# Layer 3 of a four-layer graph network: the neighbour sums as seven products of halves, with the combinations of adj made by accumulating DMAs

## The chip, the cores and the metric

The kernel runs on one core of one Trainium2 chip. A core has a matrix engine (PE, fed by weight loads PEld), three engines for elementwise work (DVE, ACT and POOL, which is GpSimd) and a queue engine SP that issues transfers. All transfers, whichever engine issues them, run on the core's 16 DMA engines. The metric is the device time of one execution in microseconds, as a median over runs.

## The reference

The input is x (16 graphs of 1024 nodes with 256 features) and adj (16 dense matrices of 1024 by 1024). Four layers follow one another; each takes h = relu(layernorm(x)), computes a graph function of h and adj, and adds it to x. The change is in the last one, layer 3:

```
h = relu(layernorm(x))
agg = epsilon * h + adj @ h                     # the sums over neighbours
g = silu(rmsnorm(agg @ W1 + b1))                # inner product, 256 -> 1024
x = x + g @ W2 + b2                             # outer product, 1024 -> 256
```

Everything is float32. epsilon * h is had by adding epsilon to adj's diagonal.

## The kernel before, in words

Layer 3 is written out for 16 batches (graphs) in `layer_3`, one after the other, with the stages of two neighbouring batches interleaved by hand. A scheduler orders each engine's instructions from that program text; every engine then works through its own queue in order, and waits where an operand or a buffer is not ready.

For one batch:

- `load(b)` (L1130) queues the loads on SP: x, h's earlier part hn, and adj transposed in two halves of 1024 rows by 512 columns, `at[b][0]` (left) and `at[b][1]` (right). A half is 2 MB, loaded by four DMAs of 512 KB (L1146). Only three buffers exist for such halves (two named bxt, one named at), so a half of batch b+2 is loaded into a buffer that batch b or b+1 has given back.
- `prepare(b)` (L1149) adds epsilon to the diagonal blocks on POOL (L1154, four small adds for each half), adds the layer's input on DVE (L1163), takes the statistics (L1166, L1167), 1/sqrt on POOL (L83, tile rs), and normalises on ACT into h (L1173, eight instructions). POOL adds b2 to x (L1177).
- `sums(b)` (L1182) makes agg transposed, tile ag, in four parts: for each half of adj's columns and each half of the 256 features, eight matmuls of 128x512 (L1189) into one PSUM tile named ph. ACT copies each to ag (L1191). Four DVE subtractions (L1195 to L1199) make the combinations tt that the next stage needs.
- `inner(ag, tt)` (L1203) is the product with W1. It is already done as seven products of halves in place of eight (Winograd's form of Strassen's scheme): 28 matmuls of 128x512 (L1210), with DVE to combine (L1229, L1231, L1214), ACT to square (L1216) and POOL to sum the squares (L1218, tiles ss, from two buffers named sq).
- `norm` turns the sums of squares with PE (`mean`, L1250), makes 1/rms on POOL (L83, tile rms), spreads it with PE (`spread`, L1258), and multiplies and applies silu on DVE and ACT (L1261, L1262).
- `outer` (L1265) is the product with W2, also as seven products: 112 matmuls of 128x128 (L1279), with the combinations made on DVE (L1273). It uses a buffer s1 of 1 MB. `prepare(b + 2)` is put in the middle of it.
- The result is stored by one DMA issued on POOL (L1337).

In iteration b the order of work is: inner of b, then the four parts of sums of b+1 with mean and spread of b between them (parts 0, mean, 1, spread, 2, 3), then outer of b with prepare of b+2. So the sums of a batch stand in one stretch of the matrix engine's queue, between inner and outer of the batch before it. The first batch has no such cover: its sums stand alone, at the end of layer 2.

Of the kernel before, what the change touches and what calls it, by code (L numbers as in the profile page):

```python
# [9 lines left out]
F32 = mybir.dt.float32  # L10
AF = mybir.ActivationFunctionType
ALU = mybir.AluOpType
# [4 lines left out]
P = 128  # L17
B, N, D, H = 16, 1024, 256, 1024
NT = N // P
DC = D // P  # L20
# [20 lines left out]
def gnn_stack(ctx: ExitStack, tc: tile.TileContext, a: dict, out: bass.AP):  # L41
    nc = tc.nc
# [29 lines left out]
    def rows(ap):  # L72
        return ap.rearrange("(t p) d -> p t d", p=P)
# [1019 lines left out]
    def layer_3(shared, x, hn, at, h, eye):  # L1093
        with ExitStack() as st:
            wp = st.enter_context(tc.tile_pool(name="w3", bufs=1))
            big = st.enter_context(tc.tile_pool(name="big3", bufs=2))
# [16 lines left out]
            NH = 512  # L1113
# [3 lines left out]
            a11, a12, a21, a22 = (w1[:, c, p * HH * P : (p + 1) * HH * P] for p in range(2) for c in range(2))  # L1117
            nc.gpsimd.tensor_tensor(ws[:, 0], a21, a22, ALU.add)
            nc.gpsimd.tensor_tensor(ws[:, 1], ws[:, 0], a11, ALU.subtract)
            nc.gpsimd.tensor_tensor(a21, a11, a21, ALU.subtract)  # L1120
            nc.gpsimd.tensor_tensor(ws[:, 2], a12, ws[:, 1], ALU.subtract)

            wt = wp.tile([P, 3, HH, P], F32, name="wt")
# [6 lines left out]
            def load(b):  # L1130
# [7 lines left out]
                while len(at[b]) < N // NH:  # L1138
# [7 lines left out]
                        nc.sync.dma_start(half[:, t : t + 2], rows(a["adjT"][b])[:, t : t + 2, n0 : n0 + NH])  # L1146
                    at[b].append(half)

            def prepare(b):  # L1149

                def diagonal(half):
                    for t in range(half * NT // 2, (half + 1) * NT // 2):
                        own = at[b][half][:, t, t * P % NH : t * P % NH + P]
                        nc.gpsimd.tensor_tensor(own, own, eye, ALU.add)  # L1154
                part = slice(0 if b else NT - 1, NT)
                if b:
                    diagonal(0)
                    h[b] = hn[b]
                tiles = range(NT)[part]
                mv = small.tile([P, NT, 2], F32, name="mv")  # L1160
                for t in tiles[::2]:
                    two = slice(t, min(t + 2, NT))
                    nc.vector.tensor_add(x[b][:, two], x[b][:, two], hn[b][:, two])  # L1163
                    for t in range(NT)[two]:
                        st = small.tile([P, 6], F32, name="st", bufs=4)
                        nc.vector.bn_stats(st, x[b][:, t])  # L1166
                        nc.vector.bn_aggr(mv[:, t], st)  # L1167
                n = len(tiles)
                rs = inv_sqrt(small, mv[:, part, 1], LN_EPS, [P, n], "rs")
                shift = small.tile([P, n], F32, name="shift")  # L1170
                nc.vector.scalar_tensor_tensor(shift, mv[:, part, 0], -1.0, rs, op0=ALU.mult, op1=ALU.mult)
                for k, t in enumerate(tiles):
                    nc.scalar.activation(h[b][:, t], x[b][:, t], AF.Relu, bias=shift[:, k : k + 1], scale=rs[:, k : k + 1])  # L1173
                diagonal(1)
                to = x[b] if b else big.tile([P, NT, D], F32, name="x", bufs=3)
                for t in range(0, NT, 2):
                    nc.gpsimd.tensor_tensor(to[:, t : t + 2], x[b][:, t : t + 2], b2[:, None].to_broadcast([P, 2, D]), ALU.add)  # L1177
                x[b] = to

            def sums(b):  # L1180

                ag = big.tile([P, DC, N], F32, name="ag", bufs=1)  # L1182
                tt = big.tile([P, 4, NH], F32, name="tt", bufs=1)
                b21 = []

                def part(n0, c):
                    pa = psum.tile([P, NH], F32, name="ph", bufs=5)
                    for mt in range(NT):
                        nc.tensor.matmul(pa, h[b][:, mt, c * P : (c + 1) * P], at[b][n0 // NH][:, mt],  # L1189
                                         start=mt == 0, stop=mt == NT - 1)  # L1190
                    nc.scalar.copy(ag[:, c, n0 : n0 + NH], pa)  # L1191
                    if (n0, c) == (0, 1):
                        b21.append(pa)
                    if (n0, c) == (NH, 0):
                        nc.vector.tensor_sub(tt[:, 0], pa, ag[:, 0, :NH])  # L1195
                    if (n0, c) == (NH, 1):
                        nc.vector.tensor_sub(tt[:, 1], pa, tt[:, 0])
                        nc.vector.tensor_sub(tt[:, 2], pa, ag[:, 0, NH:])
                        nc.vector.tensor_sub(tt[:, 3], b21[0], tt[:, 1])  # L1199
                return (ag, tt), [lambda n0=n0, c=c: part(n0, c) for n0 in range(0, N, NH) for c in range(DC)]  # L1200

            def inner(ag, tt):

                hh = [big.tile([P, HC, NH], F32, name=f"hh{q}", bufs=1) for q in range(2)]
                ss = [small.tile([P, NH], F32, name=f"ss{q}", bufs=1) for q in range(2)]
# [2 lines left out]
                def product(lhsT, rhs, onto=None):  # L1208
                    ph = onto if onto is not None else psum.tile([P, NH], F32, name="ph", bufs=5)
                    nc.tensor.matmul(ph, lhsT, rhs, start=onto is None, stop=True, skip_group_check=onto is not None)  # L1210
                    return ph
# [9 lines left out]
                left = lambda: None  # L1221
                for k in range(HH):
                    mine = slice(k * P, (k + 1) * P)
                    p1, u2, u3 = (small.tile([P, NH], F32, name=name) for name in ("p1", "u2", "u3"))
                    ph = product(a11[:, mine], ag[:, 0, :NH])
                    nc.scalar.copy(p1, ph)
                    left()
                    ph = product(ws[:, 1, mine], tt[:, 1])
                    nc.vector.tensor_add(u2, ph, p1)  # L1229
                    ph = product(a21[:, mine], tt[:, 2])  # L1230
                    nc.vector.tensor_add(u3, ph, u2)  # L1231
                    p5 = product(ws[:, 0, mine], tt[:, 0])
                    result(HH + k, 1, p5, u3)
                    result(HH + k, 0, product(a22[:, mine], tt[:, 3]), u3)
                    result(k, 0, product(a12[:, mine], ag[:, 1, :NH]), p1)
                    left = lambda k=k, mine=mine, p5=p5, u2=u2: result(
                        k, 1, product(ws[:, 2, mine], ag[:, 1, NH:], p5), u2)
                left()
                return hh, ss

# [72 lines left out]

            load(0)
            prepare(0)
            load(1)
            ags, parts = sums(0)
            for part in parts:
                part()
            prepare(1)  # L1320
            for b in range(B):
                if b + 2 < B:
                    load(b + 2)
                hh, ss = inner(*ags)
                mean, spread = norm(hh, ss)
                parts = [lambda: None] * 4
                if b + 1 < B:
                    ags, parts = sums(b + 1)
                parts[0]()
                mean()  # L1330
                parts[1]()
                spread()
                parts[2]()
                parts[3]()

                outer(b, hh, (lambda: prepare(b + 2)) if b + 2 < B else (lambda: None))
                nc.gpsimd.dma_start(rows(out[b]), x[b])  # L1337

    layers_0_1()
    with tc.tile_pool(name="shared", bufs=2) as shared:  # L1340
# [50 lines left out]
```

## Time and profile before

| | |
|---|---|
| time, median of 3 runs | 4616.06 us (4612.09 to 4619.73) |
| profiled execution, span | 4622.5 us |
| PE, busy share of the span | 94% |
| DVE, ACT, POOL, busy share | 55%, 28%, 35% |
| layer 3, from its first matmul to the last instruction | 3334.9 to 4616.8 us of the span |
| one batch of layer 3, steady | 78.3 us |
| DMA engines, mean busy share in slices 30 to 39 of the span | 0 to 3 tenths |

The span runs from the first to the last instruction's record in the profiled execution, and the profile gives no other time of it; it is 6.4 us above the median of the runs. The profile has these parts: busy time by engine; the span in 40 slices; the DMA queues; the chain of work that ended last, which is followed back from the last instruction to whatever released it; groups of like instructions with their mean time and what ended the idle time before them; and DMA issues with the time from issue to landing. The chain can also be listed in order of time, and each engine's instructions as a timeline. In such a line the first number is the start in us from the beginning of the span, the second how long it took, then the engine (SPq and POOLq are the queues that issue transfers), the tile and the line, and xN for N instructions merged. PE records a float32 matmul as two instructions.

### The profile page before, as it was taken

How to read it: one execution, taken by the hardware profiler on the slowest of the kernel's cores; microseconds unless marked ns; L12 is line 12 of the kernel's file. 1: busy time of each engine (PE TensorE's matmuls, PEld its weight loads, DVE VectorE, ACT ScalarE, POOL GpSimd, SP SyncE). 2: the span in 40 equal slices, each digit the busy share in tenths (PEclk: the TensorE clock that was granted, in tenths of full speed). 3: DMA queues.
4: the chain of work that ended last, by engine and by line, in shares of the span. 5: the costliest groups of instructions: out<-in, count | busy, mean ns of one | idle time of the engine just before them, and what ended most of it. 6: DMA issues, size and time to landing. Idle time of an engine off the chain costs nothing. (4 is left out here: it accounts for less than half of the span.)

```text
span 4622.5 us, 54868 instructions
## 1 busy us (share of the span) xinstructions
PE 4336.9 (94%) x19223; PEld 2956.2 (64%) x19223; DVE 2535.5 (55%) x6436; ACT 1279.5 (28%) x2741; POOL 1623.5 (35%) x1914
## 2 busy tenths in 40 slices
PE   8999799999997899999999999999799999999998
PEld 4444345555554687778787878787655656565656
DVE  6667944555554344444444444445356666676765
ACT  1111111221121232323232323233234333333333
POOL 3222333433333333332332323234244444445352
PEclk9999899999998999999999999999899999999999
DMA  4333244455544644454444454542142222232310
GB/s 150 112 116 100 73 112 146 164 194 188 156 145 154 196 138 154 131 166 141 154 121 151 131 159 135 167 144 73 55 142 89 100 92 92 88 104 82 110 46 19
DMA packets 530989, 576.78 MB, mean 125 GB/s; under 512 B 42544, under 2 KB 439472, under 8 KB 528304
## 3 DMA queue, kind: packets, MB, share of 16 engines
q1 hardware_dynamic: 499536, 460.27, 32.0%
q0 software_dynamic: 31040, 111.44, 6.9%
q8 instruction: 206, 3.38, 0.3%
q14 instruction: 207, 1.70, 0.1%
HBM read 469.65 MB, written 116.65 MB: 127 GB/s over the span
## 5 line engine op out<-in xcount | busy, mean ns | idle before, releaser
L295 PE MATMUL pa<-at,h 128*128 128x512 f32 x1088 | 495.3, 608 | 33.0 <-DVE ag L300 33.0
L295 PE MATMUL pa<-at,q 128*128 128x512 f32 x960 | 423.6, 594 | 0.0
L623 PE MATMUL pf<-hb,ab 128*128 128x256 f32 x1568 | 407.9, 383 | 14.5 <-DMA hb<-hs_d 5.7
L295 PEld LDWEIGHTS pa<-at,h 128*128 128x128 f32 x1088 | 209.7, 196 | 277.6 <-issue 231.5
L735 PE MATMUL pf<-hs,wx 128*128 128x256 f32 x1536 | 348.9, 381 | 19.2 <-POOL hs L726 17.6
L735 PEld LDWEIGHTS pf<-hs,wx 128*128 128x128 f32 x1536 | 290.6, 191 | 62.5 <-POOL hs L726 19.4
L623 PEld LDWEIGHTS pf<-hb,ab 128*128 128x128 f32 x1568 | 280.3, 191 | 67.2 <-issue 14.2
L295 PEld LDWEIGHTS pa<-at,q 128*128 128x128 f32 x960 | 178.2, 190 | 215.9 <-issue 212.8
L1189 PE MATMUL ph<-bxt,hb 128*128 128x512 f32 x704 | 310.8, 597 | 3.8 <-ACT hb L1173 3.0
L1218 POOL TENSOR_TENSOR ss<-ss,sq 128x512 f32<-128x512 f32 x224 | 280.7, 1271 | 87.1 <-ACT sq L1216 83.4
L1023 POOL DMA_INDIRECT hs_d<-h,table x128 | 129.6, 1013 | 330.0 <-ACTq L1009 150.8
L1279 PEld LDWEIGHTS po<-w,hh 128*128 128x128 f32 x2048 | 235.9, 193 | 9.5 <-issue 7.2
L1279 PE MATMUL po<-w,hh 128*128 128x128 f32 x2048 | 240.1, 277 | 1.4 <-ACT hh L1262 0.7
L1189 PEld LDWEIGHTS ph<-bxt,hb 128*128 128x128 f32 x704 | 133.2, 192 | 164.7 <-issue 159.8
L740 DVE TENSOR_TENSOR gates<-pf,bias 128x512 f32<-128x512 f32 x128 | 88.3, 691 | 238.6 <-PE pf L735 238.6
L1261 DVE TENSOR_TENSOR hh<-hh,po 128x512 f32<-128x512 f32 x256 | 154.5, 681 | 96.7 <-PE po L1258 96.7
L83 POOL TENSOR_TENSOR rs<-rs_v,mhalf 128x8 f32<-128x8 f32 (+1 forms) x65 | 106.9, 1645 | 255.0 <-DVE rs_v L79 241.5
L771 PE MATMUL pf<-bd,h 128*128 128x384 f32 (+4 forms) x512 | 185.6, 454 | 5.3 <-ACT bs L610 2.8
L1216 ACT ACTIVATE sq<-hh 128x512 f32<-128x512 f32 x224 | 141.1, 630 | 164.3 <-DVE hh L1214 125.6
L830 ACT ACTIVATE r<-pr 128x256 f32<-128x256 f32 (+3 forms) x230 | 68.1, 348 | 403.5 <-PE pr L789 389.5
L1214 DVE SCALAR_TENSOR_TENSOR hh<-ph,b,u 128x512 f32<-128x512 f32 x192 | 144.0, 751 | 64.9 <-PE ph L1210 54.8
L774 DVE TENSOR_TENSOR bxt<-bxt,pf 128x384 f32<-128x384 f32 (+4 forms) x256 | 125.0, 501 | 97.0 <-PE pf L771 95.5
(296 smaller groups left out, 8473.1 us busy)
## 6 DMA issues: line engine op xcount, KB each, us to landing
at<-in_adjT SPq DMA_DIRECT2D x64, 1024.0 KB, 7.1
ab<-in_adj SPq DMA_DIRECT2D x128, 512.0 KB, 4.3
bxt<-in_adjT SPq DMA_DIRECT2D x88, 512.0 KB, 6.7
at<-in_adjT SPq DMA_DIRECT2D x40, 512.0 KB, 6.8
ad<-in_adj SPq DMA_DIRECT2D x128, 128.0 KB, 6.2
x_d<-x POOLq DMA_DIRECT2D x16, 1024.0 KB, 5.1
he_d<-h POOLq DMA_DIRECT2D x16, 1024.0 KB, 8.9
heT_d<-hT POOLq DMA_DIRECT2D x16, 1024.0 KB, 4.2
```

Of the source, the lines that this page charges most:

```text
L295: nc.tensor.matmul(pa, h[:, mt, c * P : (c + 1) * P], at[n0 // 512][:, mt], start=mt == 0, stop=mt == NT - 1)
L623: nc.tensor.matmul(pb, ab[:, jts[k]], hb[:, jts[k]], start=k == 0, stop=k == len(jts) - 1)
L735: nc.tensor.matmul(pg[:, e], wx[:, c, q * D + e * P : q * D + (e + 1) * P], self.hs[:, c], start=c == 0, stop=c == DC - 1)
L771: nc.tensor.matmul(pf, h[:, g, c * P : (c + 1) * P], bd[:, g, b0 : b0 + n, S : S + far], start=True, stop=True)
L774: return lambda: nc.vector.tensor_add(to, to, pf)
L1023: nc.gpsimd.indirect_dma_start(out=hs_d[t][g][:, :], out_offset=row(1, g, t, s), in_=h[:, g], in_offset=None)
L1189: nc.tensor.matmul(pa, h[b][:, mt, c * P : (c + 1) * P], at[b][n0 // NH][:, mt], start=mt == 0, stop=mt == NT - 1)
L1214: nc.vector.scalar_tensor_tensor(hh[q][:, k], ph, b1[:, k : k + 1], u, op0=ALU.add, op1=ALU.add)
L1216: nc.scalar.activation(sq, hh[q][:, k], AF.Square)
L1218: nc.gpsimd.tensor_tensor(ss[q], ss[q], sq, ALU.add)
L1261: nc.vector.tensor_mul(hh[q][:, k], hh[q][:, k], pr)
L1279: nc.tensor.matmul(po[:, n], left[:, c, n * P : (n + 1) * P], right[:, c], start=onto is None and n == 0 and c == 0, stop=c == HH - 1, ski ...
```

## The change

Part one: the eight products of the sums become seven. With adj transposed cut in quarters b11 (left, first 512 rows), b12 (right, first 512 rows), b21 (left, last 512 rows) and b22 (right, last 512 rows), and h cut likewise, the kernel now makes p1 = m0 b11 and adds m1 b21 onto it, then p5, p7, p6, one product with b21's combination, and one with b22 onto p7: seven groups of four matmuls of 128x512, where there were four groups of eight.

Part two: this needs three combinations of quarters of adj, each of 128 partitions by 2048 elements (1 MB): t1 = b12 + b11, t3 = b12 + b22, b11 + t3, and b21 plus that; four adds in all. They are made by DMAs from SBUF to SBUF that add onto their destination, issued on GpSimd (`add_to`). b12 is overwritten by t1, so t3 starts from a second load of b12 (two DMAs of 512 KB on SP, new L1197) into the buffer s1 that outer uses.

Part three: the combinations of h (S1, S2, S4 and a21 in place) are four new DVE instructions of 128x512 elements for each batch. Behind the products, DVE does seven combinations where it did four, and ACT three copies where it did four.

Part four: the order. The diagonal of the right half, and the DMA for t1, move from `prepare(b + 2)` to the end of iteration b, behind the store of the output on POOL's queue (`first_sum`, under `issue_after`). The DMA for t3 belongs to `inner`; those onto b11 and b21 to the first and second part of the sums. In the built program each engine has this order between inner of b and outer of b: PE: four matmuls of p1, mean, four onto p1, four of p5, spread, four of p7, four of p6, four with b21, eleven of outer, four with b22, the rest of outer. POOL: store, four diagonal adds, the DMA for t1, the first add of squares of the next inner, the DMA for t3, the other thirteen adds of squares, the DMA onto b11, rms, the DMA onto b21, four diagonal adds of a left half, rs. DVE: the four combinations of h stand at the end of outer, before its last add to x. SP: the left half of b+3 (once the buffer of b+1's right half is free), then b12 again, then x, and the right half (once the left half of the batch before it is free).

For the first batch POOL's order is: the DMA for t1 (still in layer 2), layer 2's last scatters, the combinations of the weights, the copy of x, four diagonal adds, rs of batch 1, the DMA for t3, four adds of b2 to x of batch 1, the DMA onto b11, the DMA onto b21, then the DMA for t1 of batch 1, its diagonal, the DMA for t3, two adds of squares, four diagonal adds of batch 2's left half, and the other adds of squares.

The diff:

```diff
--- before.py
+++ after.py
@@ -1117,7 +1117,7 @@
             a11, a12, a21, a22 = (w1[:, c, p * HH * P : (p + 1) * HH * P] for p in range(2) for c in range(2))
             nc.gpsimd.tensor_tensor(ws[:, 0], a21, a22, ALU.add)
             nc.gpsimd.tensor_tensor(ws[:, 1], ws[:, 0], a11, ALU.subtract)
-            nc.gpsimd.tensor_tensor(a21, a11, a21, ALU.subtract)
+            nc.gpsimd.tensor_tensor(a21, a21, a11, ALU.subtract)
             nc.gpsimd.tensor_tensor(ws[:, 2], a12, ws[:, 1], ALU.subtract)
 
             wt = wp.tile([P, 3, HH, P], F32, name="wt")
@@ -1146,15 +1146,16 @@
                         nc.sync.dma_start(half[:, t : t + 2], rows(a["adjT"][b])[:, t : t + 2, n0 : n0 + NH])
                     at[b].append(half)
 
+            def diagonal(b, half):
+                for t in range(half * NT // 2, (half + 1) * NT // 2):
+                    own = at[b][half][:, t, t * P % NH : t * P % NH + P]
+                    nc.gpsimd.tensor_tensor(own, own, eye, ALU.add)
+
             def prepare(b):
 
-                def diagonal(half):
-                    for t in range(half * NT // 2, (half + 1) * NT // 2):
-                        own = at[b][half][:, t, t * P % NH : t * P % NH + P]
-                        nc.gpsimd.tensor_tensor(own, own, eye, ALU.add)
                 part = slice(0 if b else NT - 1, NT)
                 if b:
-                    diagonal(0)
+                    diagonal(b, 0)
                     h[b] = hn[b]
                 tiles = range(NT)[part]
                 mv = small.tile([P, NT, 2], F32, name="mv")
@@ -1171,35 +1172,86 @@
                 nc.vector.scalar_tensor_tensor(shift, mv[:, part, 0], -1.0, rs, op0=ALU.mult, op1=ALU.mult)
                 for k, t in enumerate(tiles):
                     nc.scalar.activation(h[b][:, t], x[b][:, t], AF.Relu, bias=shift[:, k : k + 1], scale=rs[:, k : k + 1])
-                diagonal(1)
                 to = x[b] if b else big.tile([P, NT, D], F32, name="x", bufs=3)
                 for t in range(0, NT, 2):
                     nc.gpsimd.tensor_tensor(to[:, t : t + 2], x[b][:, t : t + 2], b2[:, None].to_broadcast([P, 2, D]), ALU.add)
                 x[b] = to
 
-            def sums(b):
+            def first_sum(b):
+                diagonal(b, 1)
+                add_to(quarters(b)[1], quarters(b)[0])
+
+            def quarters(b):
+                left, right = at[b]
+                return left[:, : NT // 2], right[:, : NT // 2], left[:, NT // 2 :], right[:, NT // 2 :]
+
+            def add_to(to, from_):
+                nc.gpsimd.dma_start(to, from_, accum_op=ALU.add)
+
+            def combined(b):
+
+                m0, m1 = h[b][:, : NT // 2], h[b][:, NT // 2 :]
+                hs = big.tile([P, 3, NT // 2, P], F32, name="hs", bufs=1)
+                t3 = big.tile([P, NT // 2, NH], F32, name="s1", bufs=1)
+                for t in range(0, NT // 2, 2):
+                    nc.sync.dma_start(t3[:, t : t + 2], rows(a["adjT"][b])[:, t : t + 2, NH:])
+                S1, S2, S4 = hs[:, 0], hs[:, 1], hs[:, 2]
+                a11, a21, a12, a22 = m0[:, :, :P], m0[:, :, P:], m1[:, :, :P], m1[:, :, P:]
+                return (t3, hs), [lambda: nc.vector.tensor_tensor(S1, a21, a22, ALU.subtract),
+                                  lambda: nc.vector.tensor_tensor(S2, S1, a11, ALU.subtract),
+                                  lambda: (nc.vector.tensor_tensor(a21, a11, a21, ALU.subtract), add_to(t3, quarters(b)[3])),
+                                  lambda: nc.vector.tensor_tensor(S4, a12, S2, ALU.add)]
+
+            def sums(b, t3, hs):
 
                 ag = big.tile([P, DC, N], F32, name="ag", bufs=1)
                 tt = big.tile([P, 4, NH], F32, name="tt", bufs=1)
-                b21 = []
-
-                def part(n0, c):
-                    pa = psum.tile([P, NH], F32, name="ph", bufs=5)
-                    for mt in range(NT):
-                        nc.tensor.matmul(pa, h[b][:, mt, c * P : (c + 1) * P], at[b][n0 // NH][:, mt],
-                                         start=mt == 0, stop=mt == NT - 1)
-                    nc.scalar.copy(ag[:, c, n0 : n0 + NH], pa)
-                    if (n0, c) == (0, 1):
-                        b21.append(pa)
-                    if (n0, c) == (NH, 0):
-                        nc.vector.tensor_sub(tt[:, 0], pa, ag[:, 0, :NH])
-                    if (n0, c) == (NH, 1):
-                        nc.vector.tensor_sub(tt[:, 1], pa, tt[:, 0])
-                        nc.vector.tensor_sub(tt[:, 2], pa, ag[:, 0, NH:])
-                        nc.vector.tensor_sub(tt[:, 3], b21[0], tt[:, 1])
-                return (ag, tt), [lambda n0=n0, c=c: part(n0, c) for n0 in range(0, N, NH) for c in range(DC)]
-
-            def inner(ag, tt):
+                b11, t1, b21, b22 = quarters(b)
+                m0, m1 = h[b][:, : NT // 2], h[b][:, NT // 2 :]
+                got = {}
+
+                def product(left, right, onto=None):
+                    pa = onto if onto is not None else psum.tile([P, NH], F32, name="ph", bufs=5)
+                    for k in range(NT // 2):
+                        nc.tensor.matmul(pa, left[:, k], right[:, k], start=onto is None and k == 0, stop=k == NT // 2 - 1,
+                                         skip_group_check=True)
+                    return pa
+
+                def room(name):
+                    return small.tile([P, NH], F32, name=name)
+
+                def first():
+                    got["p1"] = product(m0[:, :, :P], b11)
+                    got["c1"] = room("p1")
+                    nc.scalar.copy(got["c1"], got["p1"])
+                    add_to(b11, t3)
+
+                def second():
+                    product(m1[:, :, :P], b21, got["p1"])
+                    nc.scalar.copy(ag[:, 0, :NH], got["p1"])
+                    got["p5"] = product(hs[:, 0], t1)
+                    add_to(b21, b11)
+
+                def third():
+                    p7 = product(m0[:, :, P:], t3)
+                    p6 = product(hs[:, 1], b11)
+                    u2, got["u3"] = room("u2"), room("u3")
+                    nc.vector.tensor_add(u2, p6, got["c1"])
+                    nc.vector.tensor_add(got["u3"], p7, u2)
+                    nc.vector.tensor_sub(ag[:, 1, NH:], got["p5"], got["u3"])
+                    got["p7"] = p7
+
+                def fourth():
+                    pa = product(m1[:, :, P:], b21)
+                    nc.vector.tensor_add(ag[:, 1, :NH], pa, got["u3"])
+                    p7 = product(hs[:, 2], b22, got["p7"])
+                    nc.scalar.copy(tt[:, 2], p7)
+                    nc.vector.tensor_sub(tt[:, 1], ag[:, 0, :NH], p7)
+                    nc.vector.tensor_sub(tt[:, 0], ag[:, 1, NH:], tt[:, 1])
+                    nc.vector.tensor_sub(tt[:, 3], ag[:, 1, :NH], tt[:, 1])
+                return (ag, tt), [first, second, third, fourth]
+
+            def inner(ag, tt, between):
 
                 hh = [big.tile([P, HC, NH], F32, name=f"hh{q}", bufs=1) for q in range(2)]
                 ss = [small.tile([P, NH], F32, name=f"ss{q}", bufs=1) for q in range(2)]
@@ -1235,6 +1287,8 @@
                     result(k, 0, product(a12[:, mine], ag[:, 1, :NH]), p1)
                     left = lambda k=k, mine=mine, p5=p5, u2=u2: result(
                         k, 1, product(ws[:, 2, mine], ag[:, 1, NH:], p5), u2)
+                    if between:
+                        between.pop(0)()
                 left()
                 return hh, ss
 
@@ -1313,19 +1367,25 @@
 
             load(0)
             prepare(0)
+            first_sum(0)
             load(1)
-            ags, parts = sums(0)
-            for part in parts:
+            of, adds = combined(0)
+            ags, parts = sums(0, *of)
+            for part in adds + parts:
                 part()
             prepare(1)
+            first_sum(1)
             for b in range(B):
                 if b + 2 < B:
                     load(b + 2)
-                hh, ss = inner(*ags)
+                adds = []
+                if b + 1 < B:
+                    of, adds = combined(b + 1)
+                hh, ss = inner(*ags, adds)
                 mean, spread = norm(hh, ss)
                 parts = [lambda: None] * 4
                 if b + 1 < B:
-                    ags, parts = sums(b + 1)
+                    ags, parts = sums(b + 1, *of)
                 parts[0]()
                 mean()
                 parts[1]()
@@ -1334,7 +1394,10 @@
                 parts[3]()
 
                 outer(b, hh, (lambda: prepare(b + 2)) if b + 2 < B else (lambda: None))
-                nc.gpsimd.dma_start(rows(out[b]), x[b])
+                stored = nc.gpsimd.dma_start(rows(out[b]), x[b])
+                if b + 2 < B:
+                    with tc.issue_after(stored.ins):
+                        first_sum(b + 2)
 
     layers_0_1()
     with tc.tile_pool(name="shared", bufs=2) as shared:
```

## The prediction, on record before the run

> **What bounds the kernel now.** I read first the page's busy times, then the chain of work that ended last in order of time, then the timelines of POOL and SP through one batch, then the transfers. The page's first line says that the matrix engine is the one to look at:
>
> ```profile
> PE 4336.9 (94%) x19223; PEld 2956.2 (64%) x19223; DVE 2535.5 (55%) x6436; ACT 1279.5 (28%) x2741; POOL 1623.5 (35%) x1914
> ```
>
> An average over four layers doesn't settle it for layer 3. The chain in order of time does:
>
> ```profile
> 4394.21 24.04 PE ph L1210 x56
> 4418.24 6.87 PE ph L1189 x16
> 4425.11 0.87 PE po L1250 x8
> 4425.98 6.87 PE ph L1189 x16
> 4432.85 0.88 PE po L1258 x8
> 4433.73 13.73 PE ph L1189 x32
> 4447.46 25.06 PE po L1279 x224
> 4472.52 24.04 PE ph L1210 x56
> ```
>
> This is one whole batch, 4472.52 - 4394.21 = 78.31 us, and each piece starts where the one before ends: PE never waits. The sums are L1189: 6.87 + 6.87 + 13.73 = 27.47 us for 32 matmuls, 0.858 us each. Call T0 the end of inner (here 4418.24).
>
> The first batch is different. Its sums have no neighbour's work beside them:
>
> ```profile
> 3357.21 1.65 POOL at L1154 x4
> 3358.86 10.49 issue
> 3369.35 0.02 POOLq L1177
> 3369.37 0.02 issue
> 3369.39 1.67 POOL rs L83
> ...
> 3374.75 25.45 PE ph L1210 x54
> ```
>
> Here the second matmul of inner starts at 3374.75 because a chain over loads, POOL's rs and ACT ends only then.
>
> [...] In the built program the DMA onto b21 does wait for the one onto b11. The nearest rows of before are plain stores of 1 MB:
>
> ```profile
> heT_d<-hT POOLq DMA_DIRECT2D x16, 1024.0 KB, 4.2
> out<-x POOLq DMA_DIRECT2D x16, 1024.0 KB, 5.2
> ```
>
> The first has the shape wanted (8 KB in each partition). At the 437 GB/s that the transfer view shows while it runs, 1 MB takes 2.4 us, so 4.2 us is 1.8 us fixed and 2.4 us of data.
>
> **The change part by part.** Let X be one accumulating DMA from issue to landing.
>
> (1) PE loses four matmuls a batch: 4 x 0.858 = 3.43 us, all on the path. The sums take 24.04 us.
>
> (2) The unknown, X. Lower end 4.2 us (the second read costs nothing). Nearest estimate[...]: 1.8 + 2 x 2.4 = 6.6, and I take 6.5. Upper end, if read, read and write of a descriptor follow one another: 1.8 + 3 x 2.4 = 9.0.
>
> (3) The steady batch. Where do the deadlines lie? PE's new order, from T0: p1 to 3.43, mean to 4.30, m1 b21 to 7.73, p5 to 11.16, spread to 12.03, p7 to 15.46, p6 to 18.9, then the product with b21. POOL may issue the DMA onto b11 only behind the last add of squares:
>
> ```profile
> 4417.32 5.07 POOL L1218 TENSOR_TENSOR ss<-ss,sq 128x512 f32<-128x512 f32 x4 [0.93 <-ACT sq L1216]
> 4427.16 1.65 POOL L83 TENSOR_TENSOR rms<-rms_v,mhalf 128x8 f32<-128x8 f32 x1 [4.77 <-DVE rms_v L81]
> ```
>
> That is 4422.39, T0 + 4.15. Mean needs the same add: its second half can start at 4.25 and not at 3.87, a new stall of 0.4 us, which moves all later times by 0.4. So b11 lands at 4.2 + X (p6 needs it at 15.9: fine up to 11.6), and b21 at 4.3 + 2X, needed at 19.3. The stall is 2X - 15.0, nothing up to X = 7.5. At 6.5 there are 2 us to spare. Rms stands between the two DMAs on POOL but is ready by about T0 + 8.6, before b11 has landed. Behind the waiting DMA onto b21 stand only the diagonal adds of a left half, whose load can't start before T0 + 28, and rs, due at T0 + 45. The DMAs for t1 and t3 are issued about 7 and 9 us into inner, which lasts 24, and are needed at T0 + 7.7 and T0 + 4.2: 25 and 19 us later, cover enough.
>
> (4) The queues. POOL between store and squares: four diagonal adds (4 x 0.44 = 1.75 us) and two DMA issues (0.93 us each, as the store's): 3.6 us. Today the fourteen adds take 17.8 us in a stretch of 21.4 (4400.96 to 4422.39), so 3.6 us of slack swallow it, and the last four still start when their squares come (T0 - 0.9). DVE: 7 x 0.69 = 4.8 us more in 75, most of it beside PE; the four at the end of outer start behind the last normalisation (4472.39) and push inner's first combination 1.2 us back, while PE first needs it 5.2 us into inner (five buffers). The p7 tile must be read by DVE before b22 is added onto it: ready T0 + 24.5, needed 25.2. SP: the left buffer is now given back at T0 + 22.3 instead of 14.6, and the right at 28 as before; the right half is needed only at the end of outer, T0 + 51, and a half takes 8.5 us. The second load of b12 (1 MB) runs in the second half of outer. All at nothing, if these covers hold.
>
> So a steady batch saves 3.43 - 0.4 = 3.03, and 15 batches 45.5 us.
>
> (5) The first batch. In POOL's new queue the DMA for t3 stands behind rs of batch 1. That rs waits for statistics that wait for a load; it ends at about 3370.4, 0.6 earlier than today as DVE loses a step. Then: t3 lands 3376.9 (the four adds to x in between end by 3376.1), b11 at 3383.4, b21 at 3390.0; PE makes 3.43 with b21 and 3.43 with b22, to 3396.9, and ACT and DVE need 1.5 for tt. Inner's second matmul starts at about 3398.4 instead of 3374.75: 23.7 us late. Before the third add of squares POOL now also waits for batch 2's left half, whose load starts behind batch 1's right half, itself held until b21's product has freed its buffer (3393.5): 5 MB and the accumulates, at some 400 GB/s till about 3412, where the squares wanted POOL by 3408.5. I put 2.5 us on that. Loss 26 us, and 3 us more for each us of X above 6.5.
>
> **Sum:** gain = 45.5 - 15 x max(0, 2X - 15) - 26 - 3(X - 6.5). At X = 6.5: 19.5 us. The profile's span would go from 4622.5 to 4603; the median run lies 6.4 below the span, and takes the same difference: 4616.1 - 19.5 = 4596.6, say **4597**.
>
> **The rivals.**
> (a) The DMAs take the place of the matmuls. The same formula with X = 9.0: stalls of 3.0 us in each of 15 batches, 45.5 - 45 - 26 - 7.5 = -33: **4649**, slower. The point of change is X = 8.0. For it: every byte is read and written within SBUF here, which no row of before shows, and packets are 8 KB.[...]
> (b) X between 7.6 and 8.3: the gain is eaten by the b21 wait and the start; **4616**, no change.
> (c) The start is hidden after all (weights and statistics end earlier than I place them, or the scatters do): 45.5 - 5, **4576**. Against: three DMAs in a row behind rs are 19.5 us that nothing covers.
> (d) POOL's queue: issuing an accumulate takes POOL 2 us or more, squares pile up (two sq buffers), ACT's copies for inner come late and PE waits 1 to 2 us in each inner: 4616 - 19.5 + 15 x 1.5 = **4619**, the same within the measurement. Against: the issue of the 8 KB shape took 0.58 us, of the 1 KB shape 0.93.
>
> **How the numbers follow.** Forecast (X below 7.6) 0.43, (c) 0.04, (b) 0.09, (d) 0.05, (a) and beyond 0.39. Faster by over 0.2% (about 9 us, what a measurement of this kernel can tell from no change) is the forecast and (c): 0.47; within 0.2%: 0.14; slower: 0.39. Range: the forecast's own is 4590 to 4601 for X of 4.2 to 7.6, with a few us for the estimate of the start 4584 to 4606. The upper end must take in (a) to X = 9.5 (2 x 9.5 - 15 = 4.0 us of stall, -50 us): 4666. Below 4584 and above 4666 I leave some 0.2.
>
> **What would show it.** The seven-product pieces in the chain should add up to 24.0 us and inner and outer stay at 24.04 and 25.06. Right: the batch period is 75.3 us, no wait stands ahead of the b21 product, landing of the adding DMAs is 6 to 7 us, and inner's second matmul of batch 0 starts near 3398. Wrong by (a): an idle stretch of PE ahead of the b21 product whose releaser is a DMA, and landings above 8 us. Wrong by (d): idle PE inside inner, released by ACT or DVE, with POOL waiting for nothing. Wrong in step 5: another start of the first inner. A landing time that differs between the four DMAs would break the single X.

## The result, and the profile after

The changed kernel takes 4691.48 us (median of 4 runs, 4687.01 to 4696.95), the kernel before 4617.9 us beside it (4612.09 to 4628.8). The ratio is 1.0156, with a 95% interval of 1.0141 to 1.0171: slower by 1.6%. The profiled execution has a span of 4688.2 us, against 4622.5. The page's first line no longer looks like a matrix engine that never waits:

```profile
PE 4323.1 (92%) x19095; PEld 2939.2 (63%) x19095; DVE 2658.1 (57%) x6548; ACT 1271.6 (27%) x2725; POOL 1700.2 (36%) x1978
```

PE is busy for 13.8 us less, in a span that is 65.7 us longer (the medians differ by 73.6; the profiled execution of the kernel before lies above its median). The chain in order of time says where, in one steady batch (columns: start, us, what):

```profile
3886.75 4.05 ACT hb L1174 x8
3890.82 1.39 DVE hs L1200
3892.24 1.64 DVE hs L1201
...
3895.47 1.75 DVE hs L1203
...
3897.81 0.61 DVE u L1281
3898.47 19.62 PE ph L1262 x38
...
3925.80 6.87 PE ph L1216 x16
...
3933.55 10.30 PE ph L1216 x24
```

Before, inner was one piece of 24.04 us that followed outer directly. Now it leaves PE in the middle of outer, runs through the statistics of a later batch (DVE, and rs on POOL), its normalisation on ACT (hb, which ends 0.5 us behind outer; before, at outer's end), the four combinations of h on DVE (L1200 to L1203), and comes back to PE inside inner. The sums (L1216) are as forecast: 6.87 and 10.30 here, and 3.44 on either side. PE's timeline shows the wait (in square brackets, the idle time before an instruction and what ended it):

```profile
3898.47 2.08 PE L1262 MATMUL ph<-ag,w 128*128 128x512 f32 x2 [2.90 <-DVE u L1281]
3900.33 1.91 PE L1262 MATMUL ph<-ag,ws 128*128 128x512 f32 x2
...
3905.03 1.02 PE L1262 MATMUL ph<-tt,ws 128*128 128x512 f32 x2
```

Two things cost time here: 2.90 us of idleness ahead of the seventh matmul of inner, and then four matmuls in 6.56 us (3898.47 to 3905.03) where four take 3.43. Together that is 6.0 of the 6.2 us by which this inner is longer (30.23 against 24.03). DVE's timeline at the same time:

```profile
3890.82 1.38 DVE L1200 TENSOR_TENSOR hs<-hb 128x512 f32<-128x512 f32 x1 [3.25 <-ACT hb L1174]
3892.24 1.64 DVE L1201 TENSOR_TENSOR hs<-hs,hb 128x512 f32<-128x512 f32 x1
3893.80 1.75 DVE L1202 TENSOR_TENSOR hb<-hb 128x512 f32<-128x512 f32 x1
3895.47 1.75 DVE L1203 TENSOR_TENSOR hs<-hb,hs 128x512 f32<-128x512 f32 x1
...
3897.73 0.68 DVE L1281 TENSOR_TENSOR u<-ph,p 128x512 f32<-128x512 f32 x1
```

and POOL's:

```profile
3887.92 3.73 POOL L1177 TENSOR_TENSOR x<-x,b 128x512 f32<-128x512 f32 x3 [1.23 <-ACT hb L1174]
3891.59 1.73 POOL L1363 TENSOR_TENSOR x<-x,u 128x512 f32<-128x512 f32 x1
3893.29 1.71 POOL L1364 TENSOR_TENSOR x<-x,u 128x512 f32<-128x512 f32 x1
3894.96 1.71 POOL L1177 TENSOR_TENSOR x<-x,b 128x512 f32<-128x512 f32 x1
```

The four combinations (L1200 to L1203) take 1.38 to 1.75 us, where the prediction priced them at 0.69. They lie beside POOL's adds to x (of b2, L1177, and of outer's u, L1363 and L1364), which are longer too (1.71 to 1.73 us; the three at 3887.92 took 1.24 each). Inner's first combination, u, starts 7.5 us into inner (3897.73 - 3890.25); PE needs its result at 5.15, six matmuls behind inner's start. In the kernel before, u started 2.0 us into inner, which began at 4394.05:

```profile
4396.03 0.69 DVE L1229 TENSOR_TENSOR u<-ph,p 128x512 f32<-128x512 f32 x1 [1.03 <-PE ph L1210]
```

The adding DMAs, by tile (count, KB, median us from issue to landing):

```profile
bxt<-s POOLq DMA_DIRECT2D x11, 1024.0 KB, 6.9
bxt<-bxt POOLq DMA_DIRECT2D x17, 1024.0 KB, 7.8
s<-bxt POOLq DMA_DIRECT2D x11, 1024.0 KB, 12.4
...
at<-s POOLq DMA_DIRECT2D x5, 1024.0 KB, 7.6
at<-at POOLq DMA_DIRECT2D x5, 1024.0 KB, 7.0
at<-bxt POOLq DMA_DIRECT2D x5, 1024.0 KB, 8.4
```

Those from s go onto b11, those onto s are t3, at<-at is b21 and at<-bxt is t1; bxt<-bxt holds DMAs of both b21 and t1.

The chain through the first batch:

```profile
3364.74 7.06 DMA s<-bxt
...
3372.39 7.38 DMA bxt<-s
...
3380.31 10.86 DMA bxt<-bxt
...
3391.21 9.50 PE ph L1216 x16
...
3401.18 14.38 DMA bxt<-in_adjT
```

It is the chain that the prediction drew (rs, three adding DMAs one behind the other, two products), with longer pieces and a further wait at its end.

**The account.** From PE's timeline I take layer 3's first matmul, the start of each inner, and the time from one inner to the next (a period). The 65.7 us between the two profiled spans are made of:

| | before | after | difference | prediction |
|---|---|---|---|---|
| layer 3's first matmul, at | 3334.92 | 3327.98 | -6.9 | 0 |
| from there to the first inner | 34.03 | 72.57 | +38.5 | +23.7 (for inner's second matmul) |
| first period | 85.36 | 86.96 | +1.6 | -0.5 |
| 14 periods, mean | 78.31 | 80.55 | +31.4 in all | -42.4 |
| of a period: inner | 24.03 | 29.04 | +5.01 | 0 |
| of a period: the rest | 54.28 | 51.51 | -2.77 | -3.03 |
| last inner to the end of the span | 71.83 | 72.97 | +1.1 | 0 |

The differences add up to 65.7; the prediction's add up to -19, so it missed by 85 us. Of these, 70 are inner in 14 steady batches and 17 the first batch (to the second inner). The first line is probably not the change's: e1_inner and e6_no_b2, whose program is the same up to there, have layer 3's first matmul at 3336.6 and 3339.6 us, and over all runs below it lies between 3329 and 3346.

### The profile page after: what moved, and what is told of

The parts are those of the page before. It is cut to its first block, busy times and chain, and to the rows that moved or that the text cites. A ratio compares the mean times of both kernels' runs of the same rounds, so it can differ in the third digit from the quotient of the medians.

```text
span 4688.2 us, 55033 instructions
## 1 busy us (share of the span) xinstructions
PE 4323.1 (92%) x19095; PEld 2939.2 (63%) x19095; DVE 2658.1 (57%) x6548; ACT 1271.6 (27%) x2725; POOL 1700.2 (36%) x1978
## 3 DMA queue, kind: packets, MB, share of 16 engines
q1 hardware_dynamic: 508240, 477.05, 32.5%
## 5 line engine op out<-in xcount | busy, mean ns | idle before, releaser
L300 DVE COPY ag<-pa 128x512 f32<-128x512 f32 x64 | 44.0, 687 | 244.9 <-PE pa L295 244.7
L1316 ACT ACTIVATE hh<-hh,rw 128x512 f32<-128x512 f32 x256 | 158.7, 708 | 66.5 <-DVE hh L1315 66.5
```

Source lines behind the costliest of these rows:

```text
L1316: nc.scalar.activation(hh[q][:, k], hh[q][:, k], AF.Silu, scale=rw[:, k : k + 1])
```

## The experiments

In the expectations T1 and T2 (Theory 1 and 2) are the accounts that a run is to tell apart; each expectation says what they are in its run. In the first set T1 is that DVE's combinations of h at the end of outer keep PE waiting. Of each edit only the lines that matter are shown. `issue_after` orders an instruction behind the one named. All results in one table; ratios are to executions of the kernel before taken beside the run (medians 4617.9 to 4623.2), "start" is the time from layer 3's first matmul to the first inner, "period" the mean of the 14 periods behind the first.

| run | time, us | ratio (95%) | start | period | inner, typical |
|---|---|---|---|---|---|
| before | 4617.9 | 1 | 34.0 | 78.31 | 24.0 |
| after | 4691.5 | 1.0156 (1.0141 to 1.0171) | 72.6 | 80.55 | 29.0 |
| e1_inner | 4640.7 | 1.0041 (1.0026 to 1.0055) | 72.6 | 76.35 | 24.0 to 24.4 |
| e2_before_plus | 4644.3 | one execution | 32.5 | 79.74 | 25.1 |
| e3_no_adds | 4670.5 | one execution | 49.5 | 80.45 | 29.0 |
| e4_plain_first | 4658.3 | one execution | 32.3 | 80.63 | 29.1 |
| e5_both | 4600.7 | 0.9945 (0.9929 to 0.9962) | 32.4 | 76.64 | 24.0 to 24.4 |
| e6_no_b2 | 4630.2 | one execution | 71.1 | 75.56 | 24.0 to 24.2 |
| e7_behind_inner | 4595.4 | one execution | 34.0 | 76.53 | 24.0 |
| e10_behind_inner_timed | 4593.9 | 0.9950 (0.9934 to 0.9967) | 34.3 | 76.59 | 24.0 |
| e8_mean_later | 4643.9 | 1.0032 (1.0013 to 1.0052) | 32.2 | 78.79 | 24.0 |
| e9_b2_moved | 4586.6 | 0.9936 (0.9920 to 0.9953) | 34.0 | 75.84 | 24.0 to 24.2 |

**Which part? First set.** e1_inner puts each combination behind a group of inner, which takes them away from the end of outer:

```diff
                     if between:
-                        between.pop(0)()
+                        with tc.issue_after(made.ins):
+                            between.pop(0)()
```

> The changed kernel with its four DVE combinations of h queued inside the next inner (one behind each of its four steps), and nothing else moved. Theory 1 (late combinations: they hold back inner's first combination, PE stalls there and then runs slow for some us): the idle time ahead of the seventh matmul of inner and the slow matmuls behind it go, inner takes 24 to 25 us again and the steady period falls from 80.1 to 75.3 us; 15 x 4.8 = 72 us off the changed kernel's 4691, about 4619. Theory 2 (the accumulating DMAs and their traffic slow PE or DVE): the period stays near 80 and the time near 4690.

The idle stretch and the slow matmuls are gone, and the period falls from 80.55 to 76.35. T1 is right about the place. But 4640.7 is 22 us above its number: the period fell by 4.2 us in place of 4.8 (13 us in all), and layer 3 began 8.6 us later than in the profiled execution of the changed kernel. Against the 74.88 that 78.31 less 3.43 would give, 1.5 us of each period are still lost. The combinations still take 0.85 to 1.32 us on average (L1200 to L1203), now beside POOL's adds of squares, the last of which are late for mean (two waits of up to 0.6 us in a batch).

e2_before_plus adds four such combinations to the kernel before, with a result that nobody uses:

```diff
+                return [lambda: nc.vector.tensor_tensor(hs[:, 0], a21, a22, ALU.subtract),
+                        lambda: nc.vector.tensor_tensor(hs[:, 1], hs[:, 0], a11, ALU.subtract),
+                        lambda: nc.vector.tensor_tensor(hs[:, 2], a11, a21, ALU.subtract),
+                        lambda: nc.vector.tensor_tensor(hs[:, 3], a12, hs[:, 1], ALU.add)]
```

> The kernel before with nothing of the change but four extra DVE instructions a batch, like the changed kernel's combinations of h, written to a buffer that nobody reads; they stand at the same place, in front of the last add to x in outer. Theory 1: PE stalls about 3 us at the seventh matmul of inner, then runs slow for up to 4 us: period from 78.3 to about 83, time 4616 + 15 x 5 = about 4690. Theory 2: PE stays full and the period stays 78.3.

4644.3 lies between: neither number holds. The third of them, which needs no other, went first there, ahead of outer's end, and the rest ended sooner, as DVE's timeline of this kernel shows:

```profile
3530.86 0.88 DVE L1187 TENSOR_TENSOR hs<-hb 128x512 f32<-128x512 f32 x1 [2.14 <-ACT hb L1173]
...
3532.83 0.69 DVE L1185 TENSOR_TENSOR hs<-hb 128x512 f32<-128x512 f32 x1 [0.48 <-ACT hb L1173]
...
3535.22 1.64 DVE L1188 TENSOR_TENSOR hs<-hb,hs 128x512 f32<-128x512 f32 x1
```

Without any DMA that adds, these instructions lengthen inner by 1.1 us in most batches, and the period by 1.4 on average. And one kind of instruction, with one shape, takes 0.69 or 1.64 us: the price doesn't lie in kind and shape. That raised the question of the second set.

e3_no_adds leaves the adding DMAs out (and with them the combinations of adj), and keeps all else:

```diff
-                nc.gpsimd.dma_start(to, from_, accum_op=ALU.add)
+                pass
```

> The changed kernel without its four accumulating DMAs; the combinations of adj are left out, so the sums are of other numbers. Theory 1: inner keeps its stall and the steady period stays at about 80 us; only the first batch gains, the three waits of PE for these DMAs (24.8 + 2.5 + 7.7 us): about 4655. Theory 2: the stall in inner and the slow DVE instructions go as well, the period falls to about 75 and the time to about 4580.

Inner stays at 29.0 us, with the idle stretch and the slow matmuls. In the steady batches neither the DMAs nor their issue on POOL cost anything that can be seen. They do cost in the first batch: 23.1 us of 72.6 ahead of the first inner, and 10.6 of the first period; layer 3 began late in this run (3345.5), which is why the time itself is above T1's.

e4_plain_first sums batch 0 in eight products, as before, and all others in seven:

```diff
-            first_sum(0)
+            diagonal(0, 1)
             load(1)
-            of, adds = combined(0)
-            ags, parts = sums(0, *of)
-            for part in adds + parts:
+            ags, parts = plain_sums(0)
+            for part in parts:
```

> The changed kernel with batch 0 alone summed as before, in eight products without adding DMAs. All theories: the first batch ends as early as before, 43 us sooner (108.0 us from layer 3's first matmul to the end of the first inner go back to about 66), 4691 - 43 = about 4648; the later periods stay at 80 us.

The start is 32.3 us again. The time is 10 us above the number, of which 9 are layer 3's later begin (3336.9 against 3328.0).

**Why so dear, and do the parts add up? Second set.** e5_both is e1 and e4 together.

> The two repairs together: batch 0 summed in eight products as before, and each of the four DVE combinations of h put behind a group of inner of the batch before. If the two losses are separate places of the path (T1), the parts add: 4640.7 of the kernel with the combinations in inner, less the 42.5 us that the start costs in it (108.1 against 65.6 us from layer 3's first matmul to the end of the first inner), gives 4598, a period of 76.1 us and a start of 65.6 us. If the late start only hides waits that come back later, transfers that would then meet inner (T2), the gain of the start is partly given back and the time stays above 4615.

4600.7: T1's 4598 holds. The two losses are separate, and the kernel with both repaired is faster than the kernel before.

e6_no_b2 is the changed kernel without POOL's adds of b2 for batches 1 to 15:

```diff
-                for t in range(0, NT, 2):
+                for t in range(0, 0 if b else NT, 2):
                     nc.gpsimd.tensor_tensor(to[:, t : t + 2], x[b][:, t : t + 2], b2[:, None].to_broadcast([P, 2, D]), ALU.add)
```

> The changed kernel without POOL's four adds of b2 to x in batches 1 to 15 (that addition is left out). T1, the four combinations of h take 1.4 to 1.75 us each[...]: with at most two of POOL's five adds left beside them they take 0.7 us, two of them at most 1.7, DVE reaches the first u of inner 2 to 3.5 us earlier, the idle stretch ahead of the seventh matmul of inner falls from 2.7 us to under 1, the half-pace matmuls behind it go, and the period falls from 80.1 to about 76.5: some 4635. T2, the combinations are slow for a reason of their own (their strided operands): 1.4 to 1.75 us each, period and time as they were, 4690.

DVE's groups in the steady stretch of the changed kernel (the columns: count, busy us, mean ns of one, idle time before them):

```profile
L1202 DVE TENSOR_TENSOR hb<-hb 128x512 f32<-128x512 f32 x14 | 24.5, 1752 | 0.0
...
L1200 DVE TENSOR_TENSOR hs<-hb 128x512 f32<-128x512 f32 x14 | 19.2, 1370 | 43.3 <-ACT hb L1174 43.3
```

and of e6_no_b2:

```profile
L1200 DVE TENSOR_TENSOR hs<-hb 128x512 f32<-128x512 f32 x14 | 9.7, 692 | 43.6 <-ACT hb L1174 43.6
...
L1202 DVE TENSOR_TENSOR hb<-hb 128x512 f32<-128x512 f32 x14 | 9.6, 684 | 0.0
```

Same line, same place, same operands: 0.69 us, and the period is 75.56. T1, that POOL's adds make them dear, holds (0.7 us; the period is 0.9 us below its 76.5, the time 5 below its 4635), T2 doesn't. POOL's adds beside them are the cause, though the run doesn't show by what means: without those of b2, outer's two come earlier and POOL is through before DVE begins, as the timelines of this kernel show in one batch:

```profile
3873.26 1.27 POOL L1364 TENSOR_TENSOR x<-x,u 128x512 f32<-128x512 f32 x1
...
3875.20 0.69 DVE L1200 TENSOR_TENSOR hs<-hb 128x512 f32<-128x512 f32 x1 [3.25 <-ACT hb L1174]
```

With the idle stretch the slow matmuls went too.

**Where to put them? Third set, and the better kernel.** e7_behind_inner (with batch 0 in eight products, and the DMA for t3 left within inner) puts the combinations behind inner's last result:

```diff
-                left()
+                made = left()
+                with tc.issue_after(made.ins):
+                    for part in between:
+                        part()
```

> Batch 0 in eight products, and the four combinations of h behind the last result of inner, on a DVE that waits there for the tiles of mean; the DMA for t3 stays in inner. POOL then does only the last adds of squares beside them. T1 (only the place beside outer's end or beside POOL's full queue makes them dear): 0.7 to 0.9 us each, no idle stretch inside inner, period 75.5 us (78.14 less 3.43, and the 0.4 to 1 us by which mean waits for the squares), so 16 us below the kernel with the combinations in inner and batch 0 in eight products: about 4590. T2 (the products p5 and p6 then wait for them, or mean's reduction on DVE, behind them, comes late for spread): an idle stretch of 1 to 2 us in the sums, period 77 to 78, 4610 to 4625.

Inner is 24.0, but the combinations still take up to 1.75 us: POOL's last adds of squares stand beside them, and mean waits 1.0 us for the last of these in most batches, where it waits 0.33 to 0.57 us in e6. 76.5 us is above T1's 75.5 and below T2's 77. e10_behind_inner_timed is the same kernel in four executions:

> The kernel with the combinations behind inner's last result once more, timed: 4595.4 us in one look. If this stands, its ratio to the kernel before is 0.993 to 0.995, no better than that with the combinations inside inner (0.9945); if the single look was low, about 4600.

Its ratio, 0.9950, is that of e5_both. e8_mean_later takes that kernel and tries to cover mean's wait, by writing mean behind eight matmuls of the sums:

```diff
                 parts[0]()
-                mean()
                 parts[1]()
-                spread()
+                mean()
                 parts[2]()
+                spread()
```

> The kernel with the combinations behind inner's last result, and mean put behind the first eight matmuls of the sums in place of the first four: PE then meets mean 3.4 us later, when POOL's last add of squares (0.5 to 1 us late before) is done, and spread is still behind p5, with rms needing about 2.9 us of the 3.4 between. If the waits of mean are all that is left over 74.7 us (78.14 less 3.43): period 74.9, about 4582. If rms is not ready for spread, or POOL's DMA onto b21 comes later by this, an idle stretch of 0.5 us or more stands ahead of spread or of the product with b21, and the time is no lower than that of the kernel with mean in its old place.

It was slower than that, by 2.3 us in a period. PE's timeline shows why:

```profile
3892.72 0.44 PE L1332 MATMUL po<-ident,ss 128*128 128x128 f32 x2 [1.02 <-POOL ss L1294]
...
3896.43 0.38 PE L1332 MATMUL po<-ident,ss 128*128 128x128 f32 x2
...
3902.67 1.09 PE L1340 MATMUL po<-ident,rms 128*128 128x128 f32 x8 [1.56 <-POOL rms L83]
```

Most of mean stands where it was in PE's order, so PE waits as before, and only its last two transposes stand behind the eight matmuls, so that rms is late for spread (13 waits in the steady stretch, 25.6 us in all). This is not the order that the run was to test, and whether a later mean helps stays open.

e9_b2_moved leaves the combinations at the end of outer, as the change has them, and moves POOL's adds of b2 instead, behind the DMA onto b21 (batch 0 in eight products):

```diff
-                    add_to(b21, b11)
+                    added = add_to(b21, b11)
+                    if b > 1:
+                        with tc.issue_after(added.ins):
+                            add_b2(b)
```

> Batch 0 in eight products; the four combinations of h at the end of outer, as in the changed kernel; of POOL's queue only the adds of b2 move, from the end of outer to behind the DMA onto b21, all four of them, in batches 2 to 15. T1 (the adds of b2 beside the combinations are what made them dear): the combinations take 0.69 us, no idle stretch inside inner, period 75.45 us as in the kernel that left these adds out, and with the start of batch 0 as before the time is 4600 less 15 times 1.0, about 4586. T2 (the adds, wherever they stand, slow DVE's work beside them: here the normalisation of hh and outer's first combinations, with 5 us of adds): outer starts late or has an idle stretch of 1 to 3 us, period 77 to 78, 4610 to 4620.

DVE's timeline of this kernel, from the first combination to inner's u:

```profile
3902.19 0.69 DVE L1204 TENSOR_TENSOR hs<-hb 128x512 f32<-128x512 f32 x1 [3.25 <-ACT hb L1174]
...
3904.13 0.68 DVE L1207 TENSOR_TENSOR hs<-hb,hs 128x512 f32<-128x512 f32 x1
...
3905.33 0.68 DVE L1310 TENSOR_TENSOR u<-ph,p 128x512 f32<-128x512 f32 x1
```

Inner begins at 3901.62 here; u ends 4.4 us into it, ahead of the 5.15 at which PE needs it. 4586.6 us, 0.6% below the kernel before: T1's number (4586) holds. This is the fastest kernel of the study. Its adds of b2 now run beside DVE's normalisation, which multiplies hh in SBUF with a tile in PSUM. POOL's timeline of this kernel in the next batch:

```profile
3938.66 5.31 POOL L1181 TENSOR_TENSOR x<-x,b 128x512 f32<-128x512 f32 x4
```

DVE's timeline beside it, and behind that the one of the changed kernel, where no add of POOL stands beside these products:

```profile
3938.21 8.46 DVE L1344 TENSOR_TENSOR hh<-hh,po 128x512 f32<-128x512 f32 x14 [6.41 <-PE po L1341]
```

```profile
3933.15 9.65 DVE L1315 TENSOR_TENSOR hh<-hh,po 128x512 f32<-128x512 f32 x16 [6.41 <-PE po L1312]
```

and DVE's group of the normalisation in the steady stretch of e9_b2_moved:

```profile
L1344 DVE TENSOR_TENSOR hh<-hh,po 128x512 f32<-128x512 f32 x224 | 135.1, 678 | 89.7 <-PE po L1341 89.7
```

Four adds take 1.33 us each (1.24 alone), and DVE's products follow one another at 0.60 us with them (8.46 / 14) and without (9.65 / 16); the mean of 678 ns is what it was in the kernel before (681). So T2 falls. In these runs DVE's combinations of two tiles in SBUF were longer beside POOL's adds (1.37 to 1.75 us for 0.69), and its products with an operand in PSUM were not.

## Why the prediction was wrong

It said 4597 us, range 4584 to 4666, and faster as the likeliest sign. The time was 4691.

**Step (4) failed, in its DVE row.** It put "the four at the end of outer" at 0.69 us each, "push inner's first combination 1.2 us back, while PE first needs it 5.2 us into inner (five buffers)", and closed with "All at nothing, if these covers hold." The 0.69 came from rows whose neighbours on POOL weren't looked at. In this place four take 6.5 us, not 2.8 (four at 0.69), u starts 7.5 us into inner, and the cover is overrun by 2.4 to 2.9 us in each steady batch (batches 1 to 14). e6 shows the cause: take POOL's adds of b2 away, and the same rows are 0.69. In the batch shown DVE and POOL start one instruction each in every 1.6 to 1.7 us while both are at work; alone they take 0.69 and 1.24, together 1.93. Through what the one holds up the other, no run shows. The 1.2 us was short even at 0.69 (e9's u starts 3.7 us into inner; before, it started 2.0 us in), but that error the cover does hold. Together with the halved clock, next, this step is 70 of the 85 us of the miss.

**The same step lacked what follows a wait.** In 11 of the 14 steady batches PE ran at half its pace behind the idle stretch: 1.71 us for a matmul instead of 0.86. The trace records the TensorE clock that was granted. For the batch shown above (columns: the stretch, its length, busy us of PE, PEld, DVE, ACT and POOL with their counts, then the granted clock, the DMA share and GB/s):

```profile
3894.40:3897.70 3.30, 1.17 (x3) 0.19 (x1) 3.30 (x3) 0.00 (x0) 2.26 (x2) 1.00 0.00 0
3897.80:3904.60 6.80, 6.13 (x7) 2.41 (x8) 4.66 (x8) 2.99 (x5) 6.02 (x9) 0.50 0.73 211
3904.60:3911.40 6.80, 6.80 (x17) 3.04 (x16) 4.69 (x8) 3.01 (x5) 4.52 (x4) 1.00 1.00 200
```

The granted clock is 0.50 for 3.4 or 6.8 us in each of these 11 batches and 1.00 in the other three; in the kernel before it is 1.00 throughout from 3380 to 4570 us. In e1, e5, e6, e7 and e9 no matmul of the steady batches is slow: its two instructions take 1.02 to 1.13 us in PE's timelines, where they take 1.4 to 2.1 at half pace in the changed kernel. So the slow matmuls are the halved clock, and no steady batch of these kernels has it without the idle stretch. These halvings last 3.4 us or twice that. Two single stretches of 2.67 us were followed by one, while stretches of 2.43, 2.67 and 2.90 us, each with one of 0.5 us behind it, were not. No run set the length of a wait on purpose, so what decides between them stays open. In the three batches without the halving inner took 27.5 to 28.0 us: of its 5.0 us, some 3.7 are the idle stretches ahead of the seventh and eighth matmul, and 1.3, on average, the clock.

**Step (2), X, was right where the path depends on it, but X is not one number.** Those onto b11 took 6.9 and 7.6 us in the median and those onto b21 7.0, against 6.5 with bounds of 4.2 and 9.0; 7.0 less the 1.8 us that the prediction takes as fixed is 2.2 times its 2.4 us of data in a plain store (4.2 us, at 437 GB/s). That the 6.5 has twice the 2.4 was the author's estimate; no row of before shows it. The one for t1 takes 8.4, under a cover of 25, and the one for t3, beside x's load and the DMA for t1, 12.4, above the upper bound but under a cover of 19. **Rival (a) falls with it:** in e3 nothing changes in the steady batch when these DMAs are gone.

**Steps (1) and (3) were right:** the rest of a period loses 2.77 us, where 3.03 was forecast (mean's wait was 0.57 us in the batch shown, not 0.4).

**Step (5) had the mechanism and the wrong sizes.** Inner's second matmul comes 34.4 us later, not 23.7. Of the 10.7 between: the three DMAs took 25.3 us in place of 19.5 (5.8), the last of them 10.86; the two products took 9.5 in place of 6.9 (2.6, half pace: the granted clock was 0.50 from 3385.8 to 3396.0); t3 was issued 1.3 later; and between one landing and the next issue passed 0.57 and 0.54. Behind that the prediction had 2.5 us for POOL's wait on batch 2's left half; inner was longer by 8.5, of which 6.6 are one idle stretch. In all 42.9 us in place of 26; e4 gets nearly all of it back.

**Rival (d)** had the mark right (idle PE inside inner, released by DVE) and the cause wrong: issuing an accumulate took POOL 0.84 to 1.19 us, not 2, and in e3, without these issues, the idle stretch stays. It was priced at 1.5 us a batch, and given 0.05. No rival held that POOL's adds make DVE's combinations longer; so the range ended 25 us too low.

## What to carry to other kernels

A duration from a row holds beside the neighbours of that row: before an elementwise instruction with two SBUF operands is put somewhere, look at what POOL does in that stretch; beside POOL's adds such instructions took two to two and a half times their time here (1.37 to 1.75 us for 0.69). When the cover is short, count the wait and the matmuls behind it (here 2.4 to 2.9 us, and 3.4 or 6.8 us at half the clock behind most of them). And a step that is worth 3 us in fifteen batches may be left out of the first, which has no cover: moving four adds and leaving one batch alone turned 1.6% slower into 0.6% faster.

## What the runs showed of the hardware

- DVE's 128x512 combination of two tiles in SBUF: 0.68 to 0.69 us in e6 and e9, where POOL's adds of b2 don't stand beside it, 1.37 to 1.75 beside POOL's adds in the changed kernel; there POOL's add took 1.24 us ahead of these and 1.71 to 1.73 beside them. DVE's product with one operand in PSUM: 0.68 us in the mean, in e9 with POOL's adds of b2 beside it and in the kernel before without.
- In the changed kernel, behind 11 of 14 idle stretches of 2.43 to 2.91 us, PE's granted clock was 0.50 for 3.4 or 6.8 us, and a 128x512 float32 matmul took 1.71 us in place of 0.86. It stayed 1.00 behind stretches of 0.33 to 0.57 us that stood alone (ahead of mean). In e2 one stretch of 1.18 us with one of 0.53 behind it was followed by two matmuls of 1.76 and 1.71 us, and one of 1.20 with 0.53 behind it was not.
- An accumulating DMA of 1 MB within SBUF, in the changed kernel's steady batches: 6.9 to 8.4 us in the median, 12.4 and 12.8 beside x's load and the DMA for t1; issuing it takes POOL 0.84 to 1.19 us.
